# Layer 0's attention outputs turned to tokens before the division, with the residual given by tokens

## The chip, the cores and the metric

The kernel runs on one core of a Trainium2 chip. Five engines share the core's on-chip memory SBUF: TensorE (PE, matrix products, with PEld for its weight loads), VectorE (DVE), ScalarE (ACT), GpSimd (POOL), and SyncE (SP), which here only issues transfers. TensorE writes its results to PSUM, from which VectorE or ScalarE must fetch them. The metric is the device time of one execution in microseconds, lower is better.

## The reference

The input x has 4 images of 128 channels and 64x64 = 4096 positions. All arithmetic is in float32. Layer 0 is an attention over the positions of one image:

```
g     = groupnorm(x)
e1,e2 = prelu(w1 @ g + b1), prelu(w2 @ g + b2)     # 64 channels each
asm   = prelu(wa @ g + ba)                         # 128 channels
score = softmax(e1^T e2, over keys)                # 4096 x 4096 per image
x     = x + score @ asm
```

Layer 1 then works on tokens, that is, on x with one position per row: a layer norm, a causal attention by a running softmax with 8 heads, another layer norm, and a mixture of 64 experts. The result goes back to channels by positions. The change lies in layer 0's last line: the softmax's division, the transposition to tokens, and the addition of x.

## The kernel before

**Blocks and steps.** Layer 0 is cut into 32 blocks: 4 images (b) times 8 blocks of 512 queries (qb). A block has 16 steps (p), one for each 256 keys, so there are 512 steps in all. In each step `probs` makes scores for the *next* step (L470, into the PSUM tile `sc`, two buffers), takes the exponential (L474, ScalarE, into `pr`, three buffers) and adds it to the accumulator `acc` (L481, VectorE; in a block's first step it is copied, L478). Then `weigh` multiplies this step's `pr` with the values `am` into two PSUM banks (L494). TensorE's array is used in two halves of 64 rows, which run beside each other: one half sums over keys 0 to 63 of each group of 128 into the bank `lower`, the other over keys 64 to 127 into `upper_`. These two banks have one buffer, so the next block's first `weigh` must wait until both are emptied.

**The end of a block.** `collect` (L500) empties the banks: ScalarE copies the lower one to `o` (L504), then VectorE adds the upper one to it (L505). It also folds the two halves of `acc` (L507), takes their maximum for a later test (L509) and loads the block's x by channels into `xr` (L511, two buffers). `divide` (L514), written at step 1 of the next block, makes the row sums in every row by a product with ones (`pd`, L519), copies and adds them (L523, L524), takes their minimum for the test (L526), their reciprocal (L527), multiplies `o` by it (L528) and adds `xr` (L529). `finish` (L531), written at step 9, turns `o` to tokens by eight transposes (L538) and copies them into `t` (L540), which holds all tokens of all images for layer 1. `block_stats` (steps 11 and 12) starts layer 1's layer norm on them (L86, L87).

**The next image.** While an image is attended to, the next one is prepared: statistics of the loaded image (`stat`, L370, and L373, written at steps 1 to 9 of block 1, 8 or 16), two tiny products with the group averages at steps 11 and 13 (L377, L388), and then 16 pieces, one at each of steps 2, 6 and 10 of the blocks that follow: a projection (L415, with ScalarE's L417, VectorE's L418 and two operations more, and four SP transfers L425 and L428 that spread e1 and e2 over both row halves) or a value piece (L437). For image 0 these pieces are done at the start and in block 0. All of these, `pd` and the transposes take their PSUM from one tile `x` with a single buffer. The next image goes into `xs`, also one buffer, which is free once the last `normal` (L396) has read the one before.

**What sets the order.** In layer 0 the code only lists the work. A planner gives each engine, and SP's queue of transfers, its own order: by its own timing it takes the earliest written of what is ready. An engine then runs its queue strictly in that order, so an instruction that waits holds up all behind it. `tc.issue_after(i)` puts what is listed under it behind instruction i in that engine's queue.

After layer 0, `layer1` runs, and a test (L612 to L625) checks from `rows`, the row sums' extremes, that the exponentials without a shift stayed in range; if not, a shifted layer 0 is computed, which does not happen with these inputs.

Of the kernel before, what the change touches and what calls it, by code (L numbers as in the profile page):

```python
# [8 lines left out]
F32 = mybir.dt.float32  # L9
AF = mybir.ActivationFunctionType  # L10
ALU = mybir.AluOpType
AX = mybir.AxisListType
PSUM = bass.MemoryType.PSUM
P = 128
# [4 lines left out]
def conv_attn_hybrid_kernel(  # L19
    ctx: ExitStack,  # L20
    tc: tile.TileContext,
    x: bass.AP,
    w1t: bass.AP,
    b1: bass.AP,
# [17 lines left out]
    nc = tc.nc  # L42
# [6 lines left out]
    NCH = N // P  # L49
# [257 lines left out]

    rows = resid.tile([P, 2, B * NBLK], F32, tag="rows", name="rows")

    with ExitStack() as l0:  # L310
# [152 lines left out]
        steps = [(b, qb, p) for b in range(B) for qb in range(NBLK) for p in range(NPR)]  # L463
        acc_of, av_of = {}, {}

        def probs(b, qb, p):
            e1, e2 = queries[b, qb], keys_of[b]
            sc = ps_qk.tile([P, 2, BLK], F32, tag="qk", name=f"sc_{b}_{qb}_{p}")
            for u in range(2):
                nc.tensor.matmul(  # L470
                    sc[:, u, :], e2[halves[u], p, :], e1[halves[u], :], start=True, stop=True
                )
            pr = tmp.tile([P, 2, BLK], F32, tag="pr", name=f"pr_{b}_{qb}_{p}", bufs=3)
            nc.scalar.activation(pr, sc, AF.Exp)  # L474
            if p == 0:
                acc = small.tile([P, 2, BLK], F32, tag="acc", name=f"acc_{b}_{qb}")
                acc_of[b, qb] = acc
                nc.vector.tensor_copy(acc, pr)  # L478
            else:
                acc = acc_of[b, qb]  # L480
                nc.vector.tensor_add(acc, acc, pr)  # L481
            return pr

        def weigh(b, qb, p, pr):
# [15 lines left out]
        def collect(b, qb):  # L500

            lower, upper_ = av_of.pop((b, qb))
            o = tmp.tile([P, BLK], F32, tag="o", name=f"o_{b}_{qb}")
            nc.scalar.copy(o, lower)  # L504
            nc.vector.tensor_add(o, o, upper_)  # L505
            acc = acc_of[b, qb]
            nc.vector.tensor_add(acc[:, 0, :], acc[:, 0, :], acc[:, 1, :])  # L507
            at = b * NBLK + qb
            nc.vector.tensor_reduce(rows[:, 1, at : at + 1], acc[:, 0, :], AX.X, ALU.max)  # L509
            xr = tmp.tile([P, BLK], F32, tag="xr", name=f"xr_{b}_{qb}")  # L510
            nc.sync.dma_start(out=xr, in_=x[b, :, bass.ts(qb, BLK)])  # L511
            o_of[b, qb] = (o, xr)

        def divide(b, qb):  # L514
            o, xr = o_of[b, qb]
            acc = acc_of.pop((b, qb))
            pd = ps_x.tile([P, 2, BLK], F32, tag="x", name=f"pd_{b}_{qb}")
            for u, h in enumerate(halves):
                nc.tensor.matmul(  # L519
                    pd[:, u, :], all_ones[h, :], acc[h, 0, :], start=True, stop=True  # L520
                )
            den = tmp.tile([P, BLK], F32, tag="den", name=f"den_{b}_{qb}", bufs=1)
            nc.scalar.copy(den, pd[:, 0, :])  # L523
            nc.vector.tensor_add(den, den, pd[:, 1, :])  # L524
            at = b * NBLK + qb
            nc.vector.tensor_reduce(rows[:, 0, at : at + 1], den, AX.X, ALU.min)  # L526
            nc.vector.reciprocal(den, den)  # L527
            nc.vector.tensor_mul(o, o, den)  # L528
            nc.vector.tensor_add(o, o, xr)  # L529

        def finish(b, qb):  # L531

            o, _ = o_of.pop((b, qb))
            ptr = ps_x.tile([P, 2, BLK], F32, tag="x", name=f"otr0_{b}_{qb}")
            ptr = ptr[:, :, : BLK // 2].rearrange("p u (c d) -> p u c d", c=CPB)
            for c in range(CPB):
                for u, h in enumerate(halves):
                    nc.tensor.transpose(ptr[:, u, c, :], o[h, bass.ts(c, P)], ident[h, h])  # L538
            at = bass.ds(b * NCH + qb * CPB, CPB)
            nc.scalar.copy(  # L540
                t[:, at, :].rearrange("p c (u d) -> p c u d", u=2),
                ptr.rearrange("p u c d -> p c u d"),
            )

# [9 lines left out]
        work_off(own, 4)  # L554
        nxt = probs(*steps[0])
        done = None
        for n, (b, qb, p) in enumerate(steps):
# [12 lines left out]
            if b + 1 < B:  # L570
                if qb == q0 and 1 <= p <= len(first):
                    first[p - 1]()
                if qb == q0 and p in (11, 13):
                    last_root = chain.pop(0)()
                if qb == q0 and p == 15:
                    blocks[0][0]()
            if p == 1 and done:
                divide(*done)
            if p == 9 and done:
# [20 lines left out]
            if p == NPR - 1:  # L600
                collect(b, qb)
                done = (b, qb)
        divide(*done)
        finish(*done)
# [4 lines left out]
    def test_rows(sb, ps):  # L609

        ends = sb.tile([P, 4], F32, tag="ends", name="ends", bufs=1)
        nc.vector.tensor_reduce(ends[:, 0:1], rows[:, 0, :], AX.X, ALU.min)  # L612
        nc.vector.tensor_reduce(ends[:, 1:2], rows[:, 1, :], AX.X, ALU.max)
        nc.vector.tensor_scalar(
# [675 lines left out]
```

## Time and profile before

| | |
|---|---|
| median of 3 runs | 2492.68 us (2490.12 to 2493.69) |
| the profiled execution | 2493.74 us |
| its span, first to last instruction | 2491.7 us |
| TensorE busy | 2394.7 us, 96% of the span |
| VectorE busy | 1669.0 us, 67% |
| ScalarE busy | 1187.5 us, 48% |
| GpSimd busy | 306.3 us, 12% |
| mean granted TensorE clock | 0.985 of full |
| DMA, mean over the span | 45 GB/s |

Busy time is the time in which at least one instruction of the engine ran. Line numbers (L481) are those of the kernel before; a name such as `av<-pr,am` means that a tile av is written from pr and am. A matrix product in float32 shows as two records. A timeline's row gives the start, the length, engine, line, operation, tiles and shapes, and in brackets how long the engine had been idle and what ended that.

### The profile page before, as it was taken

To read this page: it belongs to the slowest core of one execution; us is meant where nothing else is said; L and a number is where in the kernel's file an instruction comes from. 1 tells how busy PE (TensorE), PEld (TensorE's weight loads), DVE (VectorE), ACT (ScalarE), POOL (GpSimd) and SP (SyncE) were. 2 spreads that over 40 slices of the span, in tenths; PEclk is the share of its full clock that TensorE was granted. 3 is DMA by queue.
4 is the path that set the end of the run, shared out by engine and by line. 5 is a ranking of instruction groups with operands and counts; after the bars stand their busy time and mean duration, and the time that the engine had idled before them with its cause. 6 is when DMAs were issued, how large, how long until landed. Compare 5 with 4: busy or idle time off the path is not lost.

```text
span 2491.7 us, 45505 instructions
## 1 busy us (share of the span) xinstructions
PE 2394.7 (96%) x19348; PEld 1590.2 (64%) x19348; DVE 1669.0 (67%) x2648; ACT 1187.5 (48%) x1559; POOL 306.3 (12%) x370
## 2 busy tenths in 40 slices
PE   6899999999999999999999998999999999999797
PEld 3467767577677677877777774555555555655543
DVE  6777776777766777776666666666665766766524
ACT  2344434444344444444444435666666666665341
POOL 0000000000000000000000002433333333333100
PEclk9999999999999999999999998999999999999898
DMA  3100110000100000000000001121212121121495
GB/s 98 57 17 11 28 47 9 15 18 22 47 16 9 18 11 24 17 13 5 5 9 5 9 1 35 36 53 37 53 36 53 36 53 37 36 53 37 162 348 204
DMA packets 48292, 111.03 MB, mean 45 GB/s; under 512 B 10192, under 2 KB 19024, under 8 KB 47952
## 3 DMA queue, kind: packets, MB, share of 16 engines
q1 hardware_dynamic: 46784, 107.77, 14.6%
q8 instruction: 153, 2.51, 0.4%
q14 instruction: 59, 0.48, 0.1%
q10 hardware_dynamic: 1296, 0.26, 0.1%
HBM read 86.38 MB, written 8.91 MB: 38 GB/s over the span
## 4 chain that ended last, share of the span: by engine, by line
PE 92%; DVE 4%; DMA 1%; ACT 1%; issue 1%; SPq 0%; ACTq 0%; DVEq 0%
PE av L494 34%; PE sc L470 17%; PE pk L689 9%; PE pv L807 9%; PE po L843 4%; PE pt L823 2%; PE ps L708 2%; PE pa L437 1%; PE ph L1135 1%; PE po L850 1%; PE pl L898 1%; PE pd L519 1%; PE pp L974 1%; PE pe L415 1%; DMA x<-in_x_dram 1%; PE po L1162 1%
## 5 line engine op out<-in xcount | busy, mean ns | idle before, releaser
L494 PE MATMUL av<-pr,am 64*128 64x512 f32 x4096 | 1190.3, 592 | 5.0 <-DVE o L505 5.0
L474 ACT ACTIVATE pr<-sc 128x1024 f32<-128x1024 f32 x512 | 523.9, 1023 | 706.2 <-PE sc L470 695.6
L494 PEld LDWEIGHTS av<-pr,am 64*128 64x128 f32 x4096 | 679.4, 188 | 257.8 <-issue 59.4
L481 DVE TENSOR_TENSOR acc<-acc,pr 128x1024 f32<-128x1024 f32 x480 | 585.2, 1219 | 333.3 <-ACT pr L474 321.1
L470 PE MATMUL sc<-e,e 64*128 64x512 f32 x2048 | 737.6, 594 | 0.0
L470 PEld LDWEIGHTS sc<-e,e 64*128 64x128 f32 x2048 | 352.0, 188 | 102.3 <-issue 29.1
L689 PE MATMUL pk<-xt,wks 128*128 128x512 f32 x512 | 241.9, 612 | 6.3 <-DVE inside L623 4.2
L807 PE MATMUL pv<-wvs,xt 128*128 128x512 f32 x512 | 226.9, 596 | 2.1 <-ACT v L811 2.1
L795 DVE TENSOR_TENSOR em<-em,rb 128x1024 f32<-128x1024 f32 x64 | 80.0, 1251 | 160.8 <-DMA rb<-rd 158.8
L811 ACT ACTIVATE v<-pv 128x512 f32<-128x512 f32 x256 | 152.6, 597 | 69.7 <-PE pv L807 69.7
L691 ACT ACTIVATE ks<-pk 128x512 f32<-128x512 f32 x256 | 148.6, 597 | 60.8 <-PE pk L689 60.5
L807 PEld LDWEIGHTS pv<-wvs,xt 128*128 128x128 f32 x512 | 97.0, 191 | 121.2 <-issue 115.9
L689 PEld LDWEIGHTS pk<-xt,wks 128*128 128x128 f32 x512 | 91.7, 192 | 112.8 <-issue 81.4
L697 POOL MEMSET ew<- 128x1024 f32 x1 | 1.0, 951 | 1052.2 <-PE pa L437 1052.2
L843 PEld LDWEIGHTS po<-v,em 64*64 64x64 f32 x4096 | 111.4, 133 | 26.8 <-DVE before L833 26.8
L786 POOL TENSOR_TENSOR em<-et,mask 128x1024 f32<-128x1024 f32 x64 | 120.3, 1901 | 8.1 <-ACT et L773 8.1
L843 PE MATMUL po<-v,em 64*64 64x128 f32 x4096 | 119.2, 271 | 0.0
L95 POOL TENSOR_SCALAR xg<-t,gmv,grs 128x128 f32<-128x128 f32 x120 | 94.7, 802 | 198.0 <-DVE grs L91 142.7
L527 DVE RECIPROCAL den<-den 128x512 f32<-128x512 f32 x32 | 107.3, 3353 | 1.1
L745 DVE RECIPROCAL rr<-rr 128x512 f32<-128x512 f32 x32 | 107.3, 3353 | 1.1
L730 ACT ACT_TABLE_LOAD x24 | 30.8, 1283 | 118.9 <-DVE ss L729 118.9
L731 POOL COPY state<-mm 128x1 f32<-128x1 f32 x32 | 20.6, 645 | 512.5 <-DVE mm L725 512.3
(164 smaller groups left out, 2282.3 us busy)
## 6 DMA issues: line engine op xcount, KB each, us to landing
rb<-rd SPq DMA_DIRECT2D x128, 256.0 KB
fw<-in_fw_dram SPq DMA_DIRECT2D x64, 512.0 KB
x<-in_x_dram SPq DMA_DIRECT2D x16, 512.0 KB
xr<-in_x_dram SPq DMA_DIRECT2D x32, 256.0 KB
e<-ee SPq DMA_DIRECT2D x64, 128.0 KB
out_dram<-t SPq DMA_DIRECT2D x16, 512.0 KB
e<-ee SPq DMA_DIRECT2D x64, 64.0 KB
rd<-rr SPq DMA_DIRECT2D x64, 8.0 KB
```

The lines of the kernel that those rows point to most:

```text
L470: nc.tensor.matmul(sc[:, u, :], e2[halves[u], p, :], e1[halves[u], :], start=True, stop=True)
L474: nc.scalar.activation(pr, sc, AF.Exp)
L481: nc.vector.tensor_add(acc, acc, pr)
L494: nc.tensor.matmul(av, am[h, j, :], pr[h, u, :], start=(j == 0), stop=(j == NCH - 1))
L527: nc.vector.reciprocal(den, den)
L689: nc.tensor.matmul(pk, wks[:, h, :], xt, start=True, stop=True)
L691: nc.scalar.activation(ks, pk, AF.Silu)
L745: inverse = nc.vector.reciprocal(rr, rr).ins
L786: nc.gpsimd.tensor_tensor(em, eq.unsqueeze(2).to_broadcast([P, 2 * NH, H2]), mask.unsqueeze(1).to_broadcast([P, 2 * NH, H2]), ALU.mult,)
L807: nc.tensor.matmul(pv.rearrange("p h d -> p (h d)"), xt[:, bass.ts(2 * q + s, P)], wvs[:, bass.ts(m, BLK)], start=True, stop=True,)
L811: last = nc.scalar.activation(v[:, bass.ts(m, HPB), :], pv, AF.Silu).ins
L843: nc.tensor.matmul(po[s * H2 : (s + 1) * H2, u, q, :], aas[q][half, s, h, :], vs[2 * q + s][half, h, :], start=(q == 0 and h == 0), stop=F ...
```

## The change

A new input `xtok` holds x by tokens. In each block:

- `collect` copies the upper bank to a tile `o2` on VectorE. It no longer needs ScalarE's `o` first. The copy of the next block's first exponentials into `acc` (`first_sums`), the folding of `acc` and the addition of `o2` to `o` are put behind it in VectorE's queue.
- `residual`, written at step 1, loads the block's tokens of x into their place in `t`. There is no `xr`.
- `divide` is gone. `finish` multiplies 128 columns of `acc` at a time, as stationary operand, with one column of ones, so that the row sums stand by tokens (`pd`, 8 products of one column), and transposes the undivided `o` beside them in the same PSUM tile. VectorE adds the two halves of the row sums, takes four columns' reciprocals, and for each of four groups of 128 tokens multiplies and adds to `t` in one operation.
- `rows` holds the row sums themselves, and the test takes its minimum and maximum from them.
- The next image's statistics, at the steps where they were, are each put behind the latest accumulation in VectorE's queue.

```diff
-    rows = resid.tile([P, 2, B * NBLK], F32, tag="rows", name="rows")
+    rows = resid.tile([P, B * NCH], F32, tag="rows", name="rows")
...
         def probs(b, qb, p):
...
-            if p == 0:
-                acc = small.tile([P, 2, BLK], F32, tag="acc", name=f"acc_{b}_{qb}")
-                acc_of[b, qb] = acc
-                nc.vector.tensor_copy(acc, pr)
-            else:
+            if p > 0:
                 acc = acc_of[b, qb]
-                nc.vector.tensor_add(acc, acc, pr)
+                added.append(nc.vector.tensor_add(acc, acc, pr).ins)
             return pr
+
+        def first_sums(b, qb, pr):
+            acc = small.tile([P, 2, BLK], F32, tag="acc", name=f"acc_{b}_{qb}")
+            acc_of[b, qb] = acc
+            added.append(nc.vector.tensor_copy(acc, pr).ins)
...
             o = tmp.tile([P, BLK], F32, tag="o", name=f"o_{b}_{qb}")
+            o2 = tmp.tile([P, BLK], F32, tag="o2", name=f"o2_{b}_{qb}", bufs=1)
+            acc = acc_of[b, qb]
             nc.scalar.copy(o, lower)
-            nc.vector.tensor_add(o, o, upper_)
-            acc = acc_of[b, qb]
-            nc.vector.tensor_add(acc[:, 0, :], acc[:, 0, :], acc[:, 1, :])
-            at = b * NBLK + qb
-            nc.vector.tensor_reduce(rows[:, 1, at : at + 1], acc[:, 0, :], AX.X, ALU.max)
-            xr = tmp.tile([P, BLK], F32, tag="xr", name=f"xr_{b}_{qb}")
-            nc.sync.dma_start(out=xr, in_=x[b, :, bass.ts(qb, BLK)])
-            o_of[b, qb] = (o, xr)
-
-        def divide(b, qb):
...
+            copied = nc.vector.tensor_copy(o2, upper_).ins
+
+            def fold():
+                with tc.issue_after(copied):
+                    nc.vector.tensor_add(acc[:, 0, :], acc[:, 0, :], acc[:, 1, :])
+                    nc.vector.tensor_add(o, o, o2)
+            o_of[b, qb] = o
+            return copied, fold
+
+        def residual(b, qb):
+
+            at = b * NCH + qb * CPB
+            nc.sync.dma_start(
+                out=t[:, bass.ds(at, CPB), :],
+                in_=xtok[bass.ds(at * P, CPB * P), :].rearrange("(c p) d -> p c d", p=P),
+            )
+
+        def finish(b, qb):
+
+            o = o_of.pop((b, qb))
+            acc = acc_of.pop((b, qb))
             ptr = ps_x.tile([P, 2, BLK], F32, tag="x", name=f"otr0_{b}_{qb}")
-            ptr = ptr[:, :, : BLK // 2].rearrange("p u (c d) -> p u c d", c=CPB)
+            po = ptr[:, :, : BLK // 2].rearrange("p u (c d) -> p c u d", c=CPB)
+            pd = ptr[:, :, BLK // 2 : BLK // 2 + CPB]
             for c in range(CPB):
                 for u, h in enumerate(halves):
-                    nc.tensor.transpose(ptr[:, u, c, :], o[h, bass.ts(c, P)], ident[h, h])
-            at = bass.ds(b * NCH + qb * CPB, CPB)
-            nc.scalar.copy(
-                t[:, at, :].rearrange("p c (u d) -> p c u d", u=2),
-                ptr.rearrange("p u c d -> p c u d"),
-            )
+                    nc.tensor.matmul(
+                        pd[:, u, c : c + 1], acc[h, 0, bass.ts(c, P)], ones[h, :],
+                        start=True, stop=True,
+                    )
+            for c in range(CPB):
+                for u, h in enumerate(halves):
+                    nc.tensor.transpose(po[:, c, u, :], o[h, bass.ts(c, P)], ident[h, h])
+            at = b * NCH + qb * CPB
+            sums = rows[:, bass.ds(at, CPB)]
+            nc.vector.tensor_reduce(sums, pd.rearrange("p u c -> p c u"), AX.X, ALU.add)
+            rd = small.tile([P, CPB], F32, tag="rd", name=f"rd_{b}_{qb}")
+            nc.vector.reciprocal(rd, sums)
+            for c in range(CPB):
+                to = t[:, at + c, :].rearrange("p (u d) -> p u d", u=2)
+                nc.vector.scalar_tensor_tensor(
+                    out=to, in0=po[:, c], scalar=rd[:, c : c + 1], in1=to,
+                    op0=ALU.mult, op1=ALU.add,
+                )
...
                 if qb == q0 and 1 <= p <= len(first):
-                    first[p - 1]()
+                    with tc.issue_after(added[-1]):
+                        first[p - 1]()
...
-            if p == 1 and done:
-                divide(*done)
+            if p == 1:
+                residual(b, qb)
             if p == 9 and done:
                 finish(*done)
...
             if p == NPR - 1:
-                collect(b, qb)
+                copied, fold = collect(b, qb)
+                if n + 1 < len(steps):
+                    with tc.issue_after(copied):
+                        first_sums(*steps[n + 1][:2], nxt)
+                fold()
                 done = (b, qb)
-        divide(*done)
         finish(*done)
```

## The prediction

> **What bounds the kernel now.** I read the page's slices first (TensorE at 9 tenths or more for almost the whole span), then busy time by stage, then the waits, then the timeline where waits are long. By stage, the profiled run (2493.74 us, span 2491.7) splits into start-up to the first exponential (0 to 31 us), layer 0's steps (31 to 1489.7), a seam in which layer 0 ends and layer 1 starts (1489.7 to 1501.9), and layer 1 (989.8 us), which the change does not touch. So only what shortens TensorE's layer 0, or a hole in it, is worth anything.
>
> The waits, longest first (engine, tile, line, releaser: total us, times, longest):
> ```profile
> PEld av L494 <- DVE o L505: 20.0, 31, 3.4
> PEld av L494 <- ACT o L504: 15.0, 31, 0.6
> PE pa L437 <- DVE y L418: 14.6, 7, 9.4
> PE otr L538 <- DVE o L529: 7.0, 1, 7.0
> ```
> Starts of successive exponentials (L474) give the step length: 2.575 us when nothing intrudes, and 41.2 us for 16 steps. A plain block takes 42.97: step index 1 takes 3.19 (+0.615), index 2 3.43 (+0.855, the four pd matmuls), index 10 2.87 (+0.30, the eight transposes). A projection piece adds 0.855 or 0.90. Index 1 follows every block's end; over blocks 1 to 31 its excess sums to 29.9 us. Twenty-four are the bare 0.615; two are 5.13 and 5.17 (blocks 6 and 13); five are 0.78 to 1.18.
>
> An ordinary block end, VectorE and ScalarE (start, length, line, what ended the idle time):
> ```profile
> 281.75 0.69 DVE L507 TENSOR_TENSOR acc<-acc 128x512 f32<-128x512 f32 x1
> 283.54 0.58 ACT L504 COPY o<-av 128x512 f32<-128x512 f32 x1 [0.51 <-PE av L494]
> 284.16 0.69 DVE L505 TENSOR_TENSOR o<-o,av 128x512 f32<-128x512 f32 x1 [0.39 <-ACT o L504]
> 284.90 0.72 PEld L494 LDWEIGHTS av<-pr,am 64*128 64x128 f32 x5 [0.43 <-DVE o L505]
> ```
> The scores of the next step occupy TensorE from 283.35 to about 284.2, so the lower bank, free at 284.12, is free in time. The upper bank is not: the add needs ScalarE's o first and ends at 284.85. That is the 0.615.
>
> Block 6's beginning, and block 0's late part:
> ```profile
> 332.61 0.68 DVE L505 TENSOR_TENSOR o<-o,av 128x512 f32<-128x512 f32 x1
> 333.34 0.49 PEld L494 LDWEIGHTS av<-pr,am 64*128 64x128 f32 x4 [3.26 <-DVE o L505]
> ...
> 69.94 1.29 DVE L370 BATCH_NORM_STATS2 stats<-x 128x6 f32<-128x512 f32 x2 [4.36 <-DMA x<-in_x_dram]
> 72.27 3.65 DVE L370 BATCH_NORM_STATS2 stats<-x 128x6 f32<-128x512 f32 x6
> 76.93 2.08 PE L437 MATMUL pa<-was,xn 64*128 64x128 f32 x16 [9.40 <-DVE y L418]
> ```
> The next image's statistics (L370), written in the code in block 8, sit in VectorE's queue at the end of block 5 (321.5 to 327.9). They delay the accumulations, and these the release of PSUM. In block 0 they wait for an image still being loaded, with the projection's y queued behind them. The planner fronts what is ready in its own timing.
>
> **What the Trainium skill says.** "TensorE: Matmul & The Clock Gate", "What's actually happening": an idle window of about 3.4 us halves the clock until a busy one. The trace agrees: 0.5 from 333.41 for 3.41 us after block 6's hole, 10.24 us in block 0, 10.24 us at the seam. Same page, "LDWEIGHTS (loading the stationary operand)": loading costs by columns, 107 ns for 128 (columns over 1.2). The transposes' loads in one row half begin 117 to 123 ns apart: agrees. "VectorE: DVE Perf Modes", "Mode 2×_2P": a copy gets two elements a cycle only from SBUF. Agrees: 1024 elements from SBUF take 683 ns (L478), and so do 512 from PSUM (L1180). "DMA: Bandwidth & Descriptors", "Queues, rings and completion order": each DMA engine consumes descriptors in ring order, so a transfer queues behind those issued before it. No row here isolates that.
>
> **The change part by part.**
>
> A. Statistics held behind the latest accumulation. They leave blocks 0, 5 and 12 for steps 1 to 9 of blocks 1, 8 and 16. Block 0's step 9 took 14.99 where its like took 4.36: −10.6. Blocks 6 and 13: 5.13 + 5.17 − 2×0.615 = −9.1. The new place costs 0.69 per step on a VectorE whose accumulation takes 1.22 of 2.575: hidden by 1.35 us of slack; without it, the accumulations would slip, covered by three pr buffers. Sum −19.7; if the planner finds another thing to front, half.
>
> B. Upper bank copied at once. VectorE's last accumulation ends at 281.7 and nothing on it may start before the copy, except unrelated pieces. From 283.5 the copy takes 683 ns (L1180, same shape from PSUM), ending at 284.2, beside ScalarE's, with 0.05 us for the signal: the upper slot is met to within 0.1. Queued behind are the first sums (0.68), the fold (0.69) and o+o2 (0.69), until about 286.2, where the accumulation of step 1 ran from 285.65: late by 0.6, again inside pr's three buffers. Gain 31×0.615 = 19.1, plus perhaps 0.4 of the five larger ones: −19.5; low end 31×0.3 = −9, high −20.9.
>
> C. TensorE's row sums. Removed: 32×0.855 = 27.4. Added: eight matmuls of one column per block, two records each (the other 128x1 matmuls have two), so 16 records with 16 loads of 128 columns, in two row halves. One column has no row with 64 rows. Upper bound: pa has the same 16 loads with 128 columns to stream and costs 0.90. Lower: the transposes' 8 loads cost 0.30, so 0.60. I take the middle, 0.75: 32×(0.75−0.855) = −3.4 (−8.2 to +1.4). The eight transposes stay at 0.30.
>
> D. ScalarE loses two copies of 0.585 per block, VectorE six operations of 0.69+0.69+0.69+3.35+0.68+0.69, gaining the add of o and o2 (0.69), a small reduction (0.15, L989), a reciprocal of four columns (0.17, L91) and four products of 128 columns, spaced about 0.2 (from L406: 512 columns spaced 0.61). Net some 5 us per block; zero on the path, since TensorE hides both engines.
> The x slot in PSUM is single. It is now held until the fourth product: about 1.5 us after the transposes, plus up to 1.22 for an accumulation in front. The next piece follows 2.6 to 3.0 us later in 15 blocks. I take +1 in all, range 0 to 15×0.5 = 7.5.
>
> E. The seam. Now from 1489.77 (copy of o) to 1499.15 (t copied): add, pd, den, minimum, reciprocal 3.35, product, add, transposes, copy. After: both copies to 1490.4, fold to 1491.1, o+o2 to 1491.7, matmuls and transposes to about 1492.8 at half clock, reduction, reciprocal and four products to about 1493.9. −5.2 (−3 to −7); statistics and layer 1's start follow as before, the half clock too.
> ```profile
> 1492.88 3.35 DVE L527 RECIPROCAL den<-den 128x512 f32<-128x512 f32 x1
> 1497.83 0.69 PE L538 MATMUL otr<-ident,o 64*128 64x64 f32 x8 [7.05 <-DVE o L529]
> ```
>
> F. The residual's loads. xr had two buffers, so at most two were in flight. The new 32 write to t, which waits for nothing. SP's queue shows what the planner does with such loads:
> ```profile
> 7.73 0.43 SPq L110 DMA_DIRECT2D wks<-in_wkt_dram  x1
> 15.09 0.33 SPq L511 DMA_DIRECT2D xr<-in_x_dram  x1
> 24.12 1.15 SPq L425 DMA_DIRECT2D e<-ee  x2
> ```
> Layer 1's weights are written at step 16 and the second xr at step 31, yet both went out before the first e. So many token loads may too. Each is 512 packets of 512 B on 16 engines at 27 to 38 ns (this trace's packets of that size): 0.9 to 1.2 us, 32 to 37 in all. SP has room for about eight between 15.4 and 24.1. Each further one ahead of the first e delays layer 0's start by some 1.05, and the e behind them is on the path (first exponential at 31.0). The count is the planner's; 8 give 0, all 31 give +23. I take 13: +5.
>
> **Sum:** −19.7 −19.5 −3.4 +1 −5.2 +5 = −41.8. From the run's own 2493.74: 2451.9. The run lies 1.1 above the median of 2492.68, so 2452 against 2492.7, a gain of 1.6%.
>
> **Rivals.**
> 1. All loads go ahead of e: +23 in place of +5, so 2470. For it: no buffer limits them. Against: e are earlier in the code, and win when ready.
> 2. The bank is still late (the planner puts work between, or ScalarE's copy turns out to end the wait): B is lost, 2471. For it: both waits have 31 entries. Against: the lower bank is free 0.08 before its slot.
> 3. Slower: the one-column records do not overlap between row halves. At the load's full 188 ns each (mean of L494's loads) a block pays 3.0 instead of 0.855: 32×2.15 = +69, less the other parts' 38.4: 2524. It decides from 0.855 + 38.4/32 = 2.05 us per block, 0.13 per record. For it: loads of the full array (L377) begin 0.11 apart. Against: pa's halves start within 2 ns of each other.
> 4. The pin does not hold the statistics back, so A is lost: 2472. The queue order would show it.
>
> **How the numbers follow.** Forecast as summed, 2437 to 2464: 0.62. Rival 1 0.14, rivals 2 and 4 0.11, rival 3 0.06. The rest 0.07: a larger gain 0.03, about no change 0.03, slower otherwise 0.01. The range runs from 2437 (−19.7 −20.9 −8.2 −7 = −55.8, with nothing on D and F) to 2475, rivals 1, 2 and 4 with a few us more. Within 0.2% is about what a measurement can tell from no change: 0.03; slower 0.07; faster 0.90.
>
> **What would show each step.** Index 1 at about 2.6 in all blocks, 6 and 13 included (A, B); block 0's step 9 near 4.4 (A); index 2 at 2.58, and index 10 at 2.87+0.75 = 3.6 (C), pieces after it at 3.43 (D); layer 1's first pk about 12 to 13 us after the last av becomes about 7 (E); first exponential at 31 to 40 (F). The prediction is wrong if the small matmuls cost over 1 us, if the first exponential is later than 45, or if new holes open at the pieces behind the x slot.

## The result, and the profile after

| | before | after |
|---|---|---|
| median of 4 runs each | 2493.18 us (2490.12 to 2495.25) | 2461.45 us (2459.11 to 2461.83) |
| the profiled execution | 2493.74 us | 2461.61 us |
| its span | 2491.7 us | 2459.9 us |
| TensorE / VectorE / ScalarE busy | 2394.7 / 1669.0 / 1187.5 us | 2376.7 / 1519.5 / 1150.0 us |

The ratio after to before is 0.9872, with a 95% interval of 0.9855 to 0.9889: 1.3% faster, 31.7 us. The forecast was 2452, and 2437 to 2475 as range. So the sign and the range held, and the forecast promised 10 us too much (41.8 against the 31.8 by which the span shrank).

Line numbers below are those of the changed kernel (exponential L475, attention matmul L496, copies of the bank L508 and L509) unless said otherwise. The answers to the lines shown ahead of the prediction, first the waits (total us, times, longest):
```profile
DVE o L509 <- PE av L496: 60.7, 32, 2.0
PEld av L496 <- ACT o L508: 14.5, 31, 0.6
PE pa L438 <- DVE y L419: 5.9, 7, 1.5
```
The 20 us in which the attention matmuls' loads waited for VectorE's add are gone from the list, and VectorE is listed as waiting for the bank. (The list counts an engine's idle time. A wait of one row half while the other's loads run isn't in it, and such a wait is left; it comes up again under B.) The wait of a value piece for y, 14.6 us with a longest of 9.4, is down to 5.9 and 1.5. An ordinary block end in the timeline, then the load of the upper row half (the 64 rows of TensorE that write the upper bank), which the merged row hides, and last the lower row half's loads in the kernel before, at the block end shown ahead of the prediction:
```profile
321.23 0.58 ACT L508 COPY o<-av 128x512 f32<-128x512 f32 x1 [0.47 <-PE av L496]
321.45 0.69 DVE L509 COPY o<-av 128x512 f32<-128x512 f32 x1 [2.01 <-PE av L496]
321.87 1.48 PEld L496 LDWEIGHTS av<-pr,am 64*128 64x128 f32 x8 [0.42 <-ACT o L508]
322.06 0.68 DVE L484 COPY acc<-pr 128x1024 f32<-128x1024 f32 x1
322.66 0.68 DVE L513 TENSOR_TENSOR acc<-acc 128x512 f32<-128x512 f32 x1
323.26 0.68 DVE L514 TENSOR_TENSOR o<-o,o 128x512 f32<-128x512 f32 x1
```
```profile
322.20 0.18 PEld L496 LDWEIGHTS av<-pr,am 64*128 64x128 f32 x1
```
```profile
284.18 0.29 PEld L494 LDWEIGHTS av<-pr,am 64*128 64x128 f32 x2 [0.46 <-ACT o L504]
```
The two copies run side by side where copy and add stood one behind the other. The lower row half's loads begin 0.64 us after the first copy began, as before (284.18 after 283.54). The upper row half's begin 0.97 us after it, where they took 1.36 (284.90). The rest of VectorE's work stands behind, as planned.

In block 0 the statistics are gone, and something else appears. SP's queue and TensorE:
```profile
41.18 1.27 SPq L429 DMA_DIRECT2D e<-ee  x2
42.49 9.41 SPq L521 DMA_DIRECT2D t<-in_xtok_dram  x11
52.00 1.43 SPq L426 DMA_DIRECT2D e<-ee  x2
58.61 2.10 PE L471 MATMUL sc<-e,e 64*128 64x512 f32 x4 [3.13 <-DMA e<-ee]
```
Eleven token loads are issued in a row, over 9.41 us. The tile ee that the transfers at 52.00 carry was finished at 45.96 (VectorE wrote it in 0.69 us from 45.27); SP's queue holds them until 52.00, and TensorE ends up waiting for them. The seam, VectorE and TensorE:
```profile
1462.61 0.44 PE L541 MATMUL otr<-ident,o 64*128 64x64 f32 x8
1463.74 1.12 DVE L549 SCALAR_TENSOR_TENSOR t<-otr,rd,t 128x128 f32<-128x128 f32 x4
1467.76 1.08 PE L703 MATMUL pk<-xt,wks 128*128 128x512 f32 x1
```
The copies begin at 1460.12, the tokens are finished at 1464.86, and layer 1's first projection (pk) begins at 1467.76. Before, these stood at 1489.77, 1499.15 and 1501.91.

By stage, from the starts of the exponentials in the two traces ("blocks 1 to 31" runs from block 1's first exponential to layer 0's last one, the seam from there to the first pk):

| | before | after | difference |
|---|---|---|---|
| start to the first exponential | 31.03 | 31.73 | +0.7 |
| block 0 | 69.72 | 63.77 | −5.95 |
| blocks 1 to 31 | 1385.79 | 1361.41 | −24.4 |
| seam | 15.38 | 10.85 | −4.5 |
| layer 1 | 989.79 | 992.12 | +2.3 |

Within blocks 1 to 31, step index 1 (the second step of each block) lost 23.9 us in all, index 2 lost 26.6 (pd), index 10 gained 26.2 (the new row sums), and the other thirteen indices changed by less than 0.1 in sum.

### The profile page after: what moved, and what is told of

Same layout as the page of the kernel before. It is cut to its first block, busy times and chain, and to the rows that moved or that the text cites. A ratio compares the mean times of both kernels' runs of the same rounds, so it can differ in the third digit from the quotient of the medians.

```text
span 2459.9 us, 46253 instructions
## 1 busy us (share of the span) xinstructions
PE 2376.7 (97%) x19732; PEld 1610.5 (65%) x19732; DVE 1519.5 (62%) x2680; ACT 1150.0 (47%) x1495; POOL 306.3 (12%) x370
## 4 chain that ended last, share of the span: by engine, by line
PE 91%; DVE 5%; ACT 2%; DMA 1%; issue 1%; SPq 0%; ACTq 0%; DVEq 0%
PE av L496 35%; PE sc L471 18%; PE pk L703 9%; PE pv L821 8%; PE po L857 4%; PE pt L837 2%; PE ps L722 2%; PE ph L1149 1%; PE otr L535 1%; PE pa L438 1%; PE po L864 1%; PE pe L416 1%; PE pp L988 1%; PE pl L912 1%; PE po L1176 1%; PE otr L1190 1%
## 5 line engine op out<-in xcount | busy, mean ns | idle before, releaser
L496 PE MATMUL av<-pr,am 64*128 64x512 f32 x4096 | 1093.5, 591 | 0.0
L475 ACT ACTIVATE pr<-sc 128x1024 f32<-128x1024 f32 x512 | 523.9, 1023 | 788.6 <-PE sc L471 719.7
L496 PEld LDWEIGHTS av<-pr,am 64*128 64x128 f32 x4096 | 669.1, 187 | 234.1 <-issue 25.8
L471 PE MATMUL sc<-e,e 64*128 64x512 f32 x2048 | 652.4, 594 | 3.1 <-DMA e<-ee 3.1
L471 PEld LDWEIGHTS sc<-e,e 64*128 64x128 f32 x2048 | 336.6, 187 | 103.3 <-issue 17.4
L745 POOL COPY state<-mm 128x1 f32<-128x1 f32 x32 | 20.6, 645 | 508.0 <-DVE mm L739 507.9
L847 DVE TENSOR_TENSOR before<-before,pt 128x128 f32<-128x128 f32 x256 | 72.6, 284 | 9.8 <-PE pt L837 3.9
```

The source lines that it names most:

```text
L471: nc.tensor.matmul(sc[:, u, :], e2[halves[u], p, :], e1[halves[u], :], start=True, stop=True)
L496: nc.tensor.matmul(av, am[h, j, :], pr[h, u, :], start=(j == 0), stop=(j == NCH - 1))
```

## Experiments

One table for all of them, since most readings are differences between its rows. The first two columns are medians and ratios to the kernel before as it ran beside them, with the 95% interval; the others are the stages of the profiled execution.

| run | us | ratio | first exponential | block 0 | blocks 1 to 31 | seam | layer 1 |
|---|---|---|---|---|---|---|---|
| before | 2493.18 | 1 | 31.03 | 69.72 | 1385.79 | 15.38 | 989.79 |
| after | 2461.45 | 0.9872 (0.9855 to 0.9889) | 31.73 | 63.77 | 1361.41 | 10.85 | 992.12 |
| bank_only | 2474.48 | 0.9920 (0.9903 to 0.9936) | 30.63 | 68.32 | 1364.39 | 17.04 | 991.90 |
| pin_only | 2477.22 | 0.9928 (0.9911 to 0.9944) | 32.52 | 59.09 | 1376.71 | 15.37 | 992.06 |
| no_pin | 2474.30 | 0.9916 (0.9900 to 0.9933) | 31.99 | 74.32 | 1364.51 | 10.85 | 992.16 |
| loads_late | 2456.97 | 0.9846 (0.9830 to 0.9863) | 33.11 | 59.08 | 1361.39 | 10.85 | 991.12 |
| swap | 2458.88 | 0.9866 (0.9850 to 0.9883) | 30.86 | 62.16 | 1363.31 | 10.80 | 989.67 |
| sums_turned | 2443.49 | 0.9796 (0.9780 to 0.9813) | 33.26 | 64.70 | 1344.21 | 11.08 | 991.61 |
| sums_twice | 2488.55 | 0.9980 (0.9971 to 0.9989) | 31.50 | 63.74 | 1389.09 | 12.89 | 990.09 |
| all3 | 2441.33 | 0.9787 (0.9771 to 0.9804) | 32.45 | 58.60 | 1346.07 | 11.04 | 991.85 |
| piece_first | 2474.51 | 0.9920 (0.9904 to 0.9937) | 33.09 | 65.73 | 1374.11 | 10.84 | 990.39 |
| turned_late | 2438.93 | 0.9783 (0.9767 to 0.9799) | 32.88 | 58.17 | 1344.18 | 11.08 | 989.58 |
| best | 2459.01 | 0.9865 (0.9848 to 0.9881) | 32.63 | 58.16 | 1364.78 | 11.08 | 988.96 |
| after_again | 2460.70 (one run) | | 33.28 | 61.79 | 1361.39 | 10.84 | 991.67 |

Blocks 1 to 31 repeat to 0.02 us where nothing in them is changed (after, after_again, loads_late), so that column can be read to a tenth. The others cannot. The first exponential varies by 2.7 us and layer 1 by 3.2 between kernels that are alike there; the last experiment takes up the second. Block 0 of the changed kernel took 63.77 us in one execution and 61.79 in the other. The rows also come from four groups of runs, and the kernel before had medians of 2493.2 to 2494.8 beside them, so a difference of 2 us between two medians says little.

### The bank emptied at once, alone (bank_only)

The kernel before with part B and nothing else (the maximum for the test also moves behind the copy, as does the copy of the first exponentials):
```diff
             nc.scalar.copy(o, lower)
-            nc.vector.tensor_add(o, o, upper_)
+            copied = nc.vector.tensor_copy(o2, upper_).ins
...
+                with tc.issue_after(copied):
+                    nc.vector.tensor_add(acc[:, 0, :], acc[:, 0, :], acc[:, 1, :])
+                    nc.vector.tensor_add(o, o, o2)
...
```


> The kernel before with part B alone: the upper bank copied at once (into den's buffer, which is idle then), first sums, fold, add and maximum queued behind the copy; divide, xr and the statistics as before. If the two emptyings of PSUM now run side by side, step index 1 falls from 3.19 to the 2.77 that the changed kernel shows, 31 times: -13.0, about -1.4 more in the five blocks with a larger excess, and in blocks 6 and 13 the fronted statistics still delay the copy, but the bank is free about 2 us sooner: -2 to -4 each. In all -18 to -22 us. Rival: the gain at index 1 came from the lighter VectorE (no reciprocal, no maximum) and not from the order: then index 1 stays near 3.19 and the time within 5 us of before.

Blocks 1 to 31 are 21.4 us shorter. Index 1 is 2.76 in place of 3.19; in blocks 6 and 13, where the statistics are in front, it is 4.21 and 3.87 in place of 7.71 and 7.75. So B works by itself, with the reciprocal and the maximum still on VectorE, and the rival is out. It also takes 7.4 us off the two blocks, most of which was booked under A.

### The pin, alone and taken away (pin_only, no_pin)

pin_only is the kernel before with part A alone; no_pin is the changed kernel without it:
```diff
-                    with tc.issue_after(added[-1]):
-                        first[p - 1]()
+                    first[p - 1]()
```


> The kernel before with part A alone: the statistics queued behind the latest accumulation. Theory: -10.6 in block 0 (step 9 from 14.99 to 4.36) and -9.1 in blocks 6 and 13 (index 1 from 7.7 to 3.19), -19.7 us in all, index 1 otherwise 3.19. Rival: block 0's hole has another cause (the image's load itself, the projection's chain) and only moves: then step 9 or a neighbour stays above 8 and the gain is 9 us or less.

> The changed kernel without part A's queueing. The queue order has the statistics back at block 0's step 9 and at the end of blocks 5 and 12. Theory: block 0 gets its hole back, +10.6 (less where the token loads had already cost time, so +6 to +11), and blocks 6 and 13 a smaller one than before, since the bank's copy follows the last accumulation directly: +1.5 to +4.5 each. In all +10 to +20 us over the changed kernel. Rival: the lighter VectorE absorbs the statistics: then within 4 us of the changed kernel.

Alone, block 0 falls by 10.63 and blocks 1 to 31 by 9.08: 19.7 us, part A to the tenth. (The median shows 17.6: this run's first exponential is 1.5 later and its layer 1 2.3 longer.) Both theories hold. Taken out of the changed kernel, the pin costs 10.55 in block 0 and 3.10 in blocks 1 to 31, 12.9 by the medians. The two parts overlap: alone they save 10.63 + 9.08 + 21.4 = 41.1 in layer 0's blocks, together (10.63 of block 0, 23.9 of index 1) 34.5, since the hole in blocks 6 and 13 can be closed only once.

### The token loads behind the exponents' inputs (loads_late)

```diff
-                residual(b, qb)
+                with tc.issue_after(last_e[0]):
+                    residual(b, qb)
```
`last_e[0]` is the latest transfer of e2 (L429) that the code has listed, so SP's queue keeps the loads behind it.

> The changed kernel with each block's token load queued on SP behind the latest transfer of e that the code has listed by then. Theory: in the changed kernel 11 token loads in a row (42.5 to 51.9 us) hold up the e of projection 3, ready at 46.0 but issued at 52.0; TensorE misses 4.3 us at block 0's step 5 and 1.0 at step 6 at half clock, and the start is 0.7 late. So block 0 falls from 63.8 to about 58.4, first exponential at 31.0, and the time by 5 to 6 us. Rival: e was late for another reason (VectorE or ScalarE in block 0): block 0 stays within 1 us of 63.8.

SP's queue in that kernel (its L427 and L522 are L426 and L521 of the changed one):
```profile
43.54 0.60 SPq L522 DMA_DIRECT2D t<-in_xtok_dram  x1
48.00 1.12 SPq L427 DMA_DIRECT2D e<-ee  x2
```
There is one load in place of eleven, e goes out at 48.00 with its ee finished at 47.97, and block 0 is 4.69 us shorter: step 5 takes 4.36 and step 6 3.47. Against the changed kernel's second execution block 0 is 2.7 us shorter, and the medians differ by 4.5. The first exponential is not earlier (33.1). The loads cost time inside block 0, and none that shows at the start.

### What is left at index 1: exchanged copies, and a piece put in front (swap, piece_first)

The first edit exchanges the engines that empty the two banks:

```diff
-            nc.scalar.copy(o, lower)
-            copied = nc.vector.tensor_copy(o2, upper_).ins
+            copied = nc.vector.tensor_copy(o2, lower).ins
+            nc.scalar.copy(o, upper_)
```


> The changed kernel, with the two copies out of the attention bank exchanged: ScalarE takes the upper half, VectorE the lower one. What is left of the excess at index 1 (2.77 us against 2.58 of a step, 0.19 per block) is put down in our theory to the order of the two: the upper half's last matmul ends about 0.1 to 0.2 us after the lower one's, and the slower of the two copies (VectorE, 0.69 us against ScalarE's 0.58) is the one that waits for it. Exchanged, the slower copy starts first and both end closer together: index 1 at 2.60 to 2.70, so 31 times 0.07 to 0.17, 2 to 5 us less than the changed kernel (about 2457 to 2459). Rival: the excess is not the end of the copies but the upper bank's own late second matmul; then index 1 stays at 2.77 and the time within 1 us of the changed kernel.

The median fell by 2.6 us, which is what the theory asked for, and the theory is wrong all the same: index 1 rose from 2.77 to 2.83 and blocks 1 to 31 by 1.9. The profiled execution gained where the edit does nothing (block 0, first exponential, layer 1: 4.9 us together), and the medians carry such chances too. A block end in this kernel:
```profile
319.24 0.69 DVE L508 COPY o<-av 128x512 f32<-128x512 f32 x1 [1.98 <-PE av L496]
319.28 0.59 ACT L509 COPY o<-av 128x512 f32<-128x512 f32 x1 [0.69 <-PE av L496]
320.08 1.13 PE L496 MATMUL av<-pr,am 64*128 64x512 f32 x4
```
Now both row halves run in step and both copies start at once. The four records of scores begin at 319.04 and 319.47, 0.43 apart, so the next record's turn (its slot) would be 319.90; VectorE's copy ends at 319.93 and the matmul begins at 320.08. So it isn't the order of the two: between the bank's last matmul (319.20 to 319.24) and the slot lie 0.67 us, and VectorE's copy alone takes 0.69, with 0.15 for the signal and the load behind it.

The second edit moves the three pieces of a block ahead of `weigh`, and the first of them from step 2 to step 0:
```diff
+            if qb > q0 and p in (0, 6, 10) and b + 1 < B and blocks:
+                blocks.pop(0)[1]()
...
             weigh(b, qb, p, pr)
...
-            if qb > q0 and p in (2, 6, 10) and b + 1 < B and blocks:
-                blocks.pop(0)[1]()
```


> The changed kernel with one edit: of the three pieces of a later image's projections that a block takes, the first is issued between the second step's scores and the block's first attention matmul (it was issued two steps later). Theory: what is left of the excess at index 1 is TensorE standing idle until the copies out of the bank have ended and been signalled, 0.19 us; a piece in that place (0.86 to 0.90 us of TensorE's work) covers it. So in the blocks with a first piece, index 1 becomes 2.58 plus 0.86 to 0.90, which is 3.43 to 3.47, and index 3 becomes 2.58: 0.19 less for each of 18 to 20 such blocks, 3.4 to 3.8 us less than the changed kernel; blocks without such a piece keep 2.77. Rival: the 0.19 is a cost of starting on new banks, not a wait for the copies: then index 1 of those blocks is 3.62 to 3.66 and nothing is gained.

At the places it speaks of, the theory holds in all 18 blocks with a first piece: index 1 is 3.43 or 3.47, which is what a piece costs anywhere, and index 3 is 2.58. Index 1 and 3 together lose 3.5 us. So the 0.19 is time in which TensorE can do other work, and the rival is out. Yet the kernel is 13 us slower than the changed one, by something neither side had expected: index 11 is 4.51 or 4.55 in 15 blocks (3.43 and 3.47 before), 16.2 us. The edit also put the third piece ahead of step 10's attention matmuls, directly behind the transposes:
```profile
219.14 1.13 DVE L549 SCALAR_TENSOR_TENSOR t<-otr,rd,t 128x128 f32<-128x128 f32 x4
220.41 0.83 PE L438 MATMUL pa<-was,xn 64*128 64x128 f32 x10 [0.17 <-DVE t L549]
```
The piece needs the single x slot in PSUM, and that is held until the fourth product has read it at 220.27. This is the prediction's term D in the open. In the changed kernel the piece comes later by one group of attention matmuls (2.575 − 0.86 of scores = 1.72 us), and here it waits 1.08, which leaves 0.6 us as cover. The traces show the same more directly: in the changed kernel the slot is free 0.67 us before such a piece begins (in 12 of the 15 blocks, 0.74 in the others), and here the piece begins 0.15 after it is free. So the cover was 0.5 to 0.6 us.

### What the row sums cost (sums_twice, sums_turned)

sums_twice issues each of the one-column matmuls a second time, to the same place:
```diff
-            for c in range(CPB):
+            for c in [*range(CPB)] * 2:
                 for u, h in enumerate(halves):
                     nc.tensor.matmul(
                         pd[:, u, c : c + 1], acc[h, 0, bass.ts(c, P)], ones[h, :],
```


> The changed kernel, with every row-sum matmul issued twice into the same place (the second overwrites the first with the same values). Theory (the loads bound it): each block is 0.84 to 0.90 us longer, all of it at index 10 (3.72 to about 4.6), 27 to 29 us in all, so about 2489. Rival (most of the 0.84 is a wait or a fixed cost of the interlude, and the matmuls themselves run beside other work): 0.1 to 0.3 us per block, under 10 us in all.

Index 10 goes from 3.72 to 4.61: 0.89 for 16 more records, 27.7 us over blocks 1 to 31. The theory holds.

sums_turned transposes the sums and leaves the addition to VectorE:
```diff
-            pd = ptr[:, :, BLK // 2 : BLK // 2 + CPB]
+            pd = ptr[:, :, BLK // 2 :].rearrange("p u (c d) -> p c u d", c=CPB)
...
-                    nc.tensor.matmul(
-                        pd[:, u, c : c + 1], acc[h, 0, bass.ts(c, P)], ones[h, :],
-                        start=True, stop=True,
-                    )
+                    nc.tensor.transpose(pd[:, c, u, :], acc[h, 0, bass.ts(c, P)], ident[h, h])
...
-            nc.vector.tensor_reduce(sums, pd.rearrange("p u c -> p c u"), AX.X, ALU.add)
+            nc.vector.tensor_reduce(sums, pd, AX.XY, ALU.add)
```


> The changed kernel, with the row sums formed in another way: the folded sums are transposed (8 transposes per block) and VectorE adds up 128 elements per row sum, in place of 16 records of one-column fp32 matmuls. Theory: a block's sums cost 0.84 us of TensorE because each of the 16 records loads 64x128 weights, whatever it multiplies; a transpose is one record with one load, so half as many loads take half the time: index 10 falls from 3.72 to about 3.3 (0.35 to 0.45 less), 32 times that is 11 to 14 us, so about 2448. Rival: the cost is a wait of the group for its operand or a fixed cost of an interlude, not its loads; then index 10 stays within 0.1 of 3.72 and the time within 3 us of the changed kernel.

The groups of instructions (count, busy us, mean ns), of the changed kernel and then of this one:
```profile
L535 PE MATMUL otr<-ones,acc 64*128 64x1 f32 x512 | 39.5, 237 | 1.4 <-DVE acc L513 1.4
```
```profile
L535 PE MATMUL otr<-ident,acc 64*128 64x64 f32 x256 | 20.8, 222 | 1.4 <-DVE acc L513 1.4
L541 DVE TENSOR_REDUCE rows<-otr 128x4 f32<-128x512 f32 x32 | 21.9, 686 | 0.6 <-PE otr L538 0.6
```
Half the records, of 64 columns each where it was one. Index 10 falls to 3.13, by 0.59, more than the 0.35 to 0.45 that half the records would give; blocks 1 to 31 lose 17.2 us. So it is not the columns multiplied that cost, but the records. A transpose's record is also the cheaper one. In one row half transposes begin 0.062 us apart, and the records of the sums 0.112; all 16 transposes begin within 0.69 us (303.61 to 304.29), where the 16 sums and 8 transposes of the changed kernel take from 303.44 to 304.80. What makes a float32 product's record dearer than a transpose's is open. VectorE's reduction grows from 0.17 to 0.69 us per block and costs TensorE next to nothing: the sum over the indices other than 1, 2 and 10 rose by 1.2 us. That is the x slot again: all of it is at index 11, and the slot is now free only about 0.2 us before the piece begins.

### Together (all3, turned_late, best)

all3 joins sums_turned, swap and loads_late; turned_late leaves swap out; best is turned_late with the pieces moved as in piece_first. No edit is new.

(The transfers "of exponentials" in the next two texts are those of e, the exponents' inputs.)

> The changed kernel with three edits together: row sums by transposes (as in the run with turned sums), the two copies exchanged, and the token loads queued behind the latest transfer of exponentials of layer 0's projections (as in the run with late loads, which took 4.5 us off). Theory: the three lie in different places (index 10, index 1, block 0) and add up: 12 plus 3 plus 4.5, about 19 us less than the changed kernel, 2442 (2437 to 2447). Rival: what one saves a later one gives back (the bank's copies and the sums meet at the same engine, VectorE, whose reduction grows from 0.11 to about 0.7 us per block): 2447 to 2452.

> The changed kernel with the row sums by transposes and the token loads queued behind the latest transfer of exponentials, without the exchange of the two copies. Theory: the exchange cost 0.06 us per block (index 1 2.83 against 2.77), so without it the time is 1.9 us below the run with all three edits: 2439 to 2440, index 1 at 2.77 and index 10 at 3.13. Rival: the exchange is neutral in the run with all three and the difference from 2441.33 is under 0.5 us.

> The changed kernel with turned sums, late token loads and the first piece moved in front of the block's first attention matmul. Theory: the three add up, 2439.5 less 3.4 to 3.8, so 2435 to 2437. Rival: the moved piece's follow-up work on ScalarE and VectorE meets the copies of the bank and the first sums there, and delays a later step by what it saves: 2438 to 2441.

all3 gave 2441.33, as expected, and its index 1 is 2.83, so the exchange costs 1.9 us there too: turned_late is 1.9 shorter in blocks 1 to 31 and took 2438.93. It is the fastest kernel of this study, 22.5 us under the changed kernel and 2.2% under the one before. best missed both figures, with 2459.01: its blocks 1 to 31 are 20.6 longer than turned_late's. The piece behind the transposes now waits 1.6 us in 15 blocks, 24.0 us in all. That is the 1.08 of piece_first and the 0.52 by which the reduction in front of the products is longer. Index 1 and 3 give back 3.5. The expectation does not reckon with where the third piece ends up, which piece_first shows.

### Layer 1's length (after_again)

> The changed kernel once more, unchanged. Layer 1 (from the first of its projection matmuls to the end) took 989.7 to 990.1 us in three of the profiled runs and 991.1 to 992.2 in seven, with the same instructions in all. Theory: which it is depends on where layer 1's start falls between the ends of the windows in which the clock is granted (0.5 to 1.2 us after one in the three, 2.1 to 3.1 us after one in the seven), and that is free to differ between two runs of one kernel: this run shows 989.5 to 990.3 if its start falls 0.4 to 1.3 after the end of a window, 991 to 992.3 if it falls 2 to 3.2 after. Rival: layer 1's time belongs to the kernel: 992.1 whatever the place.

Layer 1's instructions are the same in all fourteen profiled executions, and take 988.96 to 992.16 us. The trace records when the clock is halved. All such stretches of one execution begin on a grid of 3.413 us, to within 0.01. Sorted by where the first pk falls in that grid:

```
first pk after a grid point, us   layer 1, us   run
0.40                              990.39        piece_first
0.49                              990.09        sums_twice
1.08                              989.58        turned_late
1.15                              989.79        before
1.17                              989.67        swap
1.69                              988.96        best
2.11                              992.06        pin_only
2.19                              991.90        bank_only
2.19                              991.85        all3
2.34                              992.16        no_pin
2.36                              992.12        after
2.48                              991.61        sums_turned
2.54                              991.67        after_again
3.13                              991.12        loads_late
```
On the whole, the later the start, the shorter layer 1, down to 988.96; then comes a jump by 3.1, and the same again. Layer 1's end keeps its place in the grid to 0.5 us (0.7 to 1.2 after a point), and its length does not. The Trainium skill, "TensorE: Matmul & The Clock Gate", "What's actually happening", says that the clock follows a free-running window of 3413 ns; the trace agrees (3.413 us in every execution), and the ordering suggests what that does to a part that no edit touches. The repeat lies at 2.54 and took 991.67, as the theory has it. It doesn't refute the rival, whose 992.1 it nearly meets; that is done by pairs such as turned_late and sums_turned, which differ in SP's queue alone and take 989.58 and 991.61. Nor is it a cost of the change: swap and turned_late hold the change too and take 989.67 and 989.58. No run set the place of the start on purpose.

## Why the prediction was right, and where it was off

The forecast was −41.8 from 2493.74; the profiled execution moved by −32.1 (2461.61). By the prediction's steps:

**A, statistics held back: −19.7, right.** Block 0's step 9 took 4.36, as said (−10.63), and blocks 6 and 13 have the index 1 of their neighbours. pin_only gave 19.7 by the stages. Nothing was lost in the new place, at steps 1 to 9.

**B, the bank: −19.5, a size off.** The mechanism is right: the 20 us of waits are gone, and bank_only gains 21.4 us by it alone. But "the upper slot is met to within 0.1" was taken as a gain of the whole 0.615 per block. Index 1 is 2.77 where 2.6 was forecast: 0.19 stays, 5.95 us over 31 blocks. A and B together were to take 28.6 from index 1 and took 23.9. The upper row half runs 0.22 behind the lower, VectorE's copy of it ends at 322.15, and its matmul starts at 322.20, where its slot was at 322.12. So the slot is missed by 0.085 us, within the 0.1 that was said. The other 0.10 lies one record on: the upper row half's second matmul follows the first after 0.53 us (322.20, 322.74), where 0.43 is the rule. The kernel before shows the same 0.53 (284.90, 285.43), so of its 0.615 only 0.51 was the late add, and the prediction's "That is the 0.615" put all of it down to that. Why the second record comes late after such a stop is open. piece_first showed that all of the 0.19 can be covered with other work, and swap that it isn't a matter of which engine takes which half.

**C, row sums: −3.4, a size off.** 0.75 per block was the middle of two bounds, and 0.84 was measured (3.72 − 2.575 − 0.30), against 0.855 for what it replaced: −0.3 to −0.5 in all. The upper bound, from the value pieces with 16 records at 0.90, was the true likeness; the lower one took the eight transposes' 0.30 twice, and sums_turned shows that a transpose isn't half of such a product. The sums' records follow each other at 112 ns in a row half. The prediction's reading that the transposes' loads begin 117 to 123 ns apart in a row half took every second load: in block 5 of the kernel before they begin at 312.17, 312.23 and 312.30, 0.06 apart. Only at the seam, at half clock, are they 0.107 apart (1497.87, 1497.97, 1498.08). So its "agrees" with 107 ns holds at half clock and not at full clock; the sum did not use that figure. Rival 3, which decides from 2.05 us per block on, is far off.

**D, the x slot: +1, nothing measured.** Pieces behind it take 3.43 and 3.47 as before. The range was the right one to keep: the cover is about half a microsecond, and piece_first paid 16.2 for using it up.

**E, the seam: −5.2, came to −4.5.** The working stands, and it belongs to the new end of a block: pin_only and bank_only, which keep the old one, have seams of 15.37 and 17.04. The step that failed is "statistics and layer 1's start follow as before, the half clock too": in this pair of executions layer 1 is 2.3 us longer, and its half-clock stretches lie elsewhere. The grid accounts for that size, as far as an ordering of fourteen executions can; then it is a chance of the pair.

**F, the token loads: +5, right in size by luck, wrong in place.** Six loads went ahead of the first e, where 13 were assumed and eight were said to have room; the first exponential came at 31.7, and nothing was lost there. The other 26 stood in front of the later transfers of e, inside block 0: step 5 took 8.69 where 4.36 is the rule and step 6 4.46 in place of 3.47, 5.3 us. That size itself is not firm: the same kernel's second execution lost 2.7 us there (7.08 and 3.49). The prediction asked how many loads stand before the first e, and not whether the later e can wait: block 0's early steps use them as soon as they are there. The 0.9 to 1.2 us of the DMA engines' time per load was right, though the sums built on it are loose: 32 such loads are 29 to 38 us and not 32 to 37, and 23 further ones at 1.05 are 24, not 23. Neither moves the forecast. The busy times by stretch show it in their last two columns (DMA share and GB/s):
```profile
44.00:48.00 4.00, 3.36 (x29) 2.05 (x30) 3.90 (x6) 1.02 (x1) 0.00 (x0) 1.00 1.03 255
48.00:52.00 4.00, 3.94 (x20) 1.46 (x16) 3.21 (x6) 1.71 (x2) 0.00 (x0) 1.00 1.15 292
```
The engines are full (a share of 1.0 and more), and 256 KB at 255 to 292 GB/s take 0.9 to 1.0 us. So e was late twice: issued at 52.00 where it was ready at 45.96, and then 3.9 us from the end of its issue (54.74) to the scores at 58.61, where the kernel before took 1.3 for its first e (26.61 to 27.90) on engines that were less than half busy. The Trainium skill says in "DMA: Bandwidth & Descriptors", "Queues, rings and completion order", that each DMA engine consumes descriptors in ring order; these 3.9 us agree with a transfer that stands behind the loads, and no run takes that apart.

The misses, 4.7 (A and B at index 1), 2.9 (C), 3.0 (E), −1.0 (D) and 0.3 (F), make the 10 us. B, C and E promised too much: B took its gain as whole, C the middle of its bounds, and E a layer 1 that stays as it is. That the sum came out inside the range owes something to F, whose 5 us stood for another loss than the one that came.

## What to carry to other kernels

A buffer that two engines empty is free when the slower copy has been signalled; compare that, copy and signal together, with the time until the next writer's slot, and where it falls short by little, put other work of the waiting engine into the gap. Before moving work past a shared single buffer, look for who takes the buffer next: here about half a microsecond of cover decided between nothing and 16 us. Loads with a free place to go to went out here as early as their queue let them, eleven in a row in front of a transfer on the path; tie such loads behind the transfers that the path needs.

## What the runs showed of the hardware

- The halved-clock stretches of an execution lie on a grid of 3.413 us, and the program's place in that grid differs from one execution to the next. A part with holes can end on that grid: layer 1, unchanged, took 988.96 to 992.16 us, ordered by where in the grid it began. Differences under 3 us between single executions of this kernel say nothing unless the stage is looked at.
- Float32 products of one column cost nearly what products of 128 columns cost: 0.84 to 0.89 us for 16 records on two row halves (0.112 us between records of a row half), against 0.90 for a value piece's 16. Transposes follow each other at 0.062 us, and a sum by a transpose and VectorE was 0.59 us per block cheaper on TensorE.
- The first matmul of a row half that had stopped for its bank was followed by the second after 0.53 us in place of 0.43, in both kernels.
- SP's issuing was slower when the DMA engines had been busy for long: a token load took 0.4 to 0.6 us to issue in the first rows of loads (up to 37.8 us), and 0.86 on average, 1.38 at most, in the row of eleven, with the engines at a share of 1.0 and more.
